# Layer 1 of a two-layer kernel: gating split between VectorE and GpSimd, expert sums on TensorE, and a changed order of the steps around the first and the last batches

## The chip, the core and the metric

The kernel runs on one core of a Trainium2 chip. The core has five engines, each with an instruction stream of its own that it runs in order: TensorE (PE: matrix products and transposes, with PEld for its weight loads), VectorE (DVE), ScalarE (ACT: activations), GpSimd (POOL) and SyncE (SP), which here only issues DMAs. They wait for each other through semaphores. The metric is the device time of one execution in microseconds, and the figure to compare is the median of several runs: 1055.69 us for the kernel before (3 runs, 1055.5 to 1057.73).

## What is computed

Two transformer layers over x of 8 batches x 512 tokens x 128 features, all in float32. Each layer has a mixer and a feed-forward part, both behind a layer norm that is modulated by a conditioning vector. Layer 0 is attention with low-rank weights and a mixture of experts (8 experts, 2 chosen for a token, and a shared one). Layer 1, where the change lies, is a selective state-space mixer and another mixture of experts. Cut to that:

```python
# mixer of layer 1: conv over time, projections, a linear recurrence
proj = conv(h) @ Win + b_in
delta, B_in, C = proj[..., :16], pairs_mean(proj[..., 16:48]), pairs_mean(proj[..., 48:])
dA = softplus(delta) * A                  # A = -exp(A_log)
A_bar = exp(dA)
B_bar = where(abs(A) < eps, 1 + dA / 2 + dA * dA / 6, (A_bar - 1) / A_safe) * B_in
h_t = A_bar_t * h_(t-1) + B_bar_t         # scan over 512 tokens
x = x + ga * ((C * h) @ Wout + b_out)

# feed-forward of layer 1
xc = silu(pw(conv(h)) + pw_b)
x1 = h + xc
top_v, top_i = top_k(x1 @ router_w + router_b, 2)
rw = one_hot(top_i) * softmax(top_v)      # two gates for a token, six are zero
ye = silu(x1 @ expert_w + expert_b)       # all 8 experts
moe_out = sum_e(rw[e] * ye[e]) @ out_w + out_b
h = rmsnorm(x1 + moe_out, norm_w)
x = x + gb * (h + gelu(h @ ff_down + b) @ ff_up + b2)
```

## The kernel before

Attention of layer 0 runs up to about 540 us of the profiled span and is not touched. Then a **loop over 62 blocks** does the experts of layer 0: 31 routed blocks of 256 tokens for batches 0 to 5, twelve blocks of the shared expert, fifteen routed blocks for batches 6 and 7 and their four shared ones. A pass of the loop, a *tick*, issues the transposes of the block after next, the first products of this block (`ph`, L1033, and the GELU to `hid` on ACT), and the second products of the block before (`pyb`, L1044). What layer 1 needs is put between the ticks: `when(t, do, ...)` hangs a step on tick t. `n` is 62, so ticks from n on come after the loop, and there the steps themselves are all the work. Ticks set only the order of each engine's stream; they are no times. Everything is pinned to the order in which the program issues it.

The results of routed blocks go to DRAM (`y_rows`) and come back by indirect DMAs that POOL issues, 8 per batch (`gather`, L1064); `combine` adds them on DVE. Then a batch takes these steps:

- **Mixer.** Statistics, root, centring, transposes to channels, and a convolution on DVE (`xc`). `ssm_project` (L1246) does the projections of pairs of batches; three ACT copies bring `dl`, `bi`, `ci` from PSUM. The groups (0, 1, 2, 3), (4, 5) and (6, 7) then go through a chain of seven steps: `chain_1` (L1274: bias and minus the absolute value on DVE, then exponential and logarithm on ACT), `chain_2` (on POOL the terms of the series, on ACT the exponential), `chain_3` (DVE), `chain_4` (the scan on DVE). Each switch between the tables of ACT is an instruction of its own (`ACT_TABLE_LOAD`).
- **Lead-in** (`lead_in`, L1579) for every batch: `ssm_out` (products `py`, L1327), statistics, `ffn_root` (L1336; POOL raises the variance to the power -0.5), `ffn_centre` (ACT), `ffn_channels` (transposes `ptn`), `ffn_pointwise` (L1348: products `pw`; for batches 0 to 3 SiLU is made of a hyperbolic tangent on ACT and two DVE operations into a tile `sl`, for the others it is ACT's own; POOL adds to get `x1`), `ffn_logits` (`pl`, L1371), `ffn_ranks` (comparisons on DVE, and the product `rk_eq` on POOL), `ffn_chosen`, `ffn_tanh`, `ffn_gates`, and `ffn_gates_out` (transposes `pgt`, a copy, and a DMA of the 8 x 512 gates to DRAM). The helper `later` turns estimated microseconds into ticks of 4.0 us in the loop and 2.2 us after it.
- **Experts.** `ffn_spread` (SP) reads a pair of rows of gates back, broadcast to all partitions (`gb`, 512 KB each, five buffers). For each of 8 experts `expert_in` (L1451) makes a product `pe` on PE and SiLU on ACT (`ye`), three ticks later `expert_gate` multiplies by the gates (`t`, five buffers), and `expert_sum` (L1441 in `add_up`) lets PE apply the output weights and sum the experts in PSUM (`r`). How many experts are added up on POOL before that, `sums_of` says: 2 for batches 0 to 3, 4 for batches 4 to 6, 1 for batch 7.
- **End.** Root mean square, the small feed-forward (`pf`, `pu`), and the output DMA, for batches 0 to 3 together between the experts of batches 5 and 6, then for 4 to 6, then for 7.

The first tick of a batch's experts is set by

```python
base = [n + 5 + NE * b + (5 if b > 5 else 0) for b in range(B)]
```

Of the kernel before, what the change touches and what calls it, by code (L numbers as in the profile page):

```python
# [14 lines left out]
ALU = mybir.AluOpType  # L15
# [53 lines left out]
def tile_adaln_two_blocks(  # L69
# [222 lines left out]
    with tc.tile_pool(name="at", bufs=2) as at, tc.tile_pool(name="sc", bufs=4, space=PSUM) as psc, tc.tile_pool(  # L292
# [953 lines left out]
        def ssm_project(h, s):  # L1246

            if s == 0:
                for name in ("dl", "bi", "ci"):
                    held[name] = lt([P, S], name)[0 : 16 * len(GROUPS[h]), :]  # L1250
            ps = flat(bank("pj"))
            for i in range(2):
                xc = held.pop(("xc", GROUPS[h][2 * s + i]))
                for k in range(3):
                    pin(
                        T.matmul(
                            ps[32 * k : 32 * k + 32, :],
                            lhsT=k1["wip"][:, k, i, :],
                            rhs=xc,
                            start=(i == 0),  # L1260
                            stop=(i == 1),
                        )
                    )
            for k, name in enumerate(("dl", "bi", "ci")):
                A.copy(held[name][32 * s : 32 * s + 32, :], ps[32 * k : 32 * k + 32, :])
# [8 lines left out]
        def chain_1(h, step):  # L1274

            dl = held["dl"]
            if step == 0:
                V.tensor_scalar(dl, dl, of_states(h, "bias"), None, ALU.add)
                u = chained(h, "u")
                V.scalar_tensor_tensor(u, dl, -1.0, dl, ALU.mult, ALU.min)  # L1280
            else:
                u = held["u"]
                A.activation(u, u, AF.Exp)
                A.activation(u, u, AF.Ln, bias=ones[0 : 16 * len(GROUPS[h]), 0:1])
# [63 lines left out]
        def ffn_pointwise(b):  # L1348
# [4 lines left out]
            x1 = flat(lt([P, NC4, D], "x1", tag="sh", bufs=B))  # L1353
            sl = lt([P, S], "sl", tag="xc", bufs=2)
            if b in GROUPS[0]:

                th = lt([P, S], "th", tag="gt1", bufs=2)
                A.activation(th, pw, AF.Tanh, bias=k1["pwb2"], scale=0.5)
                V.tensor_scalar(sl, pw, k1["pwb"], 0.5, ALU.add, ALU.mult)
                V.scalar_tensor_tensor(sl, th, 1.0, sl, ALU.add, ALU.mult)  # L1360
            else:
                A.activation(sl, pw, AF.Silu, bias=k1["pwb"])
            G.tensor_tensor(x1, hq[:, 2 : S + 2], sl, ALU.add)
            x1s[b] = x1
# [62 lines left out]
        def sums_of(b):  # L1427

            return 2 if b < 4 else 4 if b < B - 1 else 1

# [27 lines left out]
        def expert_gate(b, e):  # L1458
            f = ffn[b]
            t = f["t", e] = er.tile([P, S], FP, tag="t", name="t", bufs=5)  # L1460
            V.tensor_tensor(t, f.pop(("ye", e)), f["g"][e // 2][:, e % 2, :], ALU.mult)
            n = 1
# [115 lines left out]

        def lead_in(b, t):  # L1579

            when(t, ssm_out, b)
            for i in range(2):
                when(later(t, 2 * i + 1) if t >= n else t, two_stats, b, mv4, i)
            for do, us in (
                (ffn_root, 4), (ffn_centre, 8), (ffn_channels, 12), (ffn_pointwise, 16), (ffn_logits, 22),
                (ffn_ranks, 24), (ffn_chosen, 28), (ffn_tanh, 30), (ffn_gates, 32), (ffn_gates_out, 36),
            ):
                when(later(t, us), do, b)

        base = [n + 5 + NE * b + (5 if b > 5 else 0) for b in range(B)]  # L1590
        for b in range(B):
# [3 lines left out]
        for b in range(B):  # L1595
            t = base[b]
            for e in range(NE):
                when(t + e + 3, expert_gate, b, e)
            for i in range(NE // 2):
                when(max(t - 3 + 2 * i, n + 5), ffn_spread, b, i)  # L1600
            when(t - 1, ffn_residual, b)
            when(t + 5, ffn_bias, b)
            every = sums_of(b)
            lag = 4 if every == 1 else 5 if every == 2 else 6
            when(t + every - 1 + lag, sum_begin, b)
# [17 lines left out]
        for b, ts in enumerate(  # L1623
# [3 lines left out]
                (41, 42, 43, 44, 45, 46, 49),  # L1627
                (43, 44, 45, 46, 47, 48, 50),
                (46, 47, 48, 49, 50, 51, 52),
                (49, 50, 51, 52, 53, 54, 55),  # L1630
            )
# [12 lines left out]
        when(44, ssm_project, 0, 0)  # L1644
        when(49, ssm_project, 0, 1)
        when(53, out_weights, 0)
        chain(0, 50, (0, 0, 1, 2, 3, 3, 4))
        for b in GROUPS[0]:
            lead_in(b, 55 + b)
        when(59, ssm_project, 1, 0)  # L1650


        for k in range(2 * PC[1]):
            when(n - 2 + k // 3, gather, PB[0] + k // 8, k % 8)
        when(n + 8, out_weights, 1)
        chain(1, n + 5, (0, 1, 2, 4, 6, 7, 8))
        lead_in(4, n + 14)
        lead_in(5, n + 18)
        for b, t in ((6, n + 10), (7, n + 13)):
            for c in range(NC4):  # L1660
# [8 lines left out]
            when(t + 11, ssm_channels, b)  # L1669
        when(n + 20, out_weights, 2)  # L1670
        when(n + 27, ssm_project, 2, 0)
        chain(2, n + 28, (0, 1, 2, 4, 6, 7, 8))
        lead_in(6, n + 37)
        lead_in(7, n + 44)

# [111 lines left out]
```

## Time and profile before

| | us |
|---|---|
| median of 3 runs (1055.5 to 1057.73) | 1055.69 |
| the profiled execution | 1081.55 |
| its span, from first to last instruction | 1079.6 |
| PE busy in the span (93%) | 1004.6 |
| DVE busy (62%) | 668.8 |
| ACT busy (59%) | 637.0 |
| POOL busy (45%) | 486.7 |
| last products of the loop of layer 0 end at | 861.1 |
| first expert of layer 1 on PE begins at | 870.9 |
| first gated product on DVE begins at | 885.0 |
| first expert of batches 1, 2, 3, 4 begins at | 893.9 (with the last of batch 0), 919.9, 948.5 (with the last of batch 2), 972.8 (with the last of batch 3) |
| first expert of batch 6 begins at | 1030.9 |

The profile is one execution with the hardware's profiler on. A group of instructions is given with its line, engine, operation and tiles, how often it ran, its busy time, the mean length of one, and the idle time of its engine just before it with what ended that. L65 stands for most operations, as a helper records them; there the tiles tell which one it is. A matmul in float32 is two passes, so each `T.matmul` appears as two records. PE runs them in a pipeline: the mean length of one is longer than the distance from one to the next. A busy share is an average over stages with different limits, and the clock granted to PE (1.0 is full) differs by stage as well. The profiled execution is 25.9 us longer than the median of the runs.

### The profile page before, as it was taken

The numbers are of one execution on the slowest core, as the hardware profiler recorded it, in microseconds if no ns is written. First come the engines' busy times: TensorE is split into PE (matmuls) and PEld (weight loads), VectorE is DVE, ScalarE is ACT, GpSimd is POOL, SyncE is SP. The second block draws the span as 40 slices with busy tenths as digits, with TensorE's granted clock in tenths as the row PEclk, the third lists the DMA queues.
The fourth block names the chain that finished last, engine by engine and source line by source line (L and its number), as shares of the span: only waits on it lengthen the run. The fifth ranks groups of instructions, "written<-read, shape, count | busy, mean of one in ns | idle before, by whom it ended". The sixth has DMA issues, their size and how long they took to land.

```text
span 1079.6 us, 24180 instructions
## 1 busy us (share of the span) xinstructions
PE 1004.6 (93%) x9522; PEld 658.2 (61%) x9522; DVE 668.8 (62%) x1297; ACT 637.0 (59%) x1400; POOL 486.7 (45%) x764
## 2 busy tenths in 40 slices
PE   9999999999999999999989999869899967767988
PEld 7555555555555555555579899748778634344556
DVE  6967787777768777777321123035766359888663
ACT  1466676666767666676745656225586563675554
POOL 3313142554627445454453133546441374666662
PEclk9999999999999999999999999969999968999999
DMA  6099200000000000000237796412553043213051
GB/s 168 20 315 283 88 12 2 11 22 2 31 1 20 13 9 24 2 30 10 71 114 221 230 275 196 127 35 64 146 152 89 8 131 99 79 59 126 23 186 39
DMA packets 94769, 95.36 MB, mean 88 GB/s; under 512 B 7664, under 2 KB 72560, under 8 KB 94656
## 3 DMA queue, kind: packets, MB, share of 16 engines
q1 hardware_dynamic: 90384, 85.13, 26.4%
q0 software_dynamic: 4096, 8.40, 2.6%
q8 instruction: 75, 1.23, 0.5%
q10 hardware_dynamic: 176, 0.30, 0.1%
q14 instruction: 38, 0.31, 0.1%
HBM read 62.43 MB, written 31.36 MB: 87 GB/s over the span
## 4 chain that ended last, share of the span: by engine, by line
PE 75%; DVE 10%; POOL 5%; ACT 4%; issue 4%; DMA 1%; SPq 0%; DVEq 0%; ACTq 0%; POOLq 0%
PE ps L531 21%; PE av L552 11%; PE pyb L1044 9%; PE ph L1033 8%; PE pm L484 3%; PE pmt L519 2%; PE r L1441 2%; PE pw L1352 2%; PE ppt L570 2%; DVE t L65 1%; DVE xc L65 1%; PE idle L417 1%; PE pe L1453 1%; PE pqk L444 1%; PE pyb L1003 1%
## 5 line engine op out<-in xcount | busy, mean ns | idle before, releaser
L65 DVE TENSOR_REDUCE mpad<-pm 128x2 f32<-128x1024 f32 (+1 forms) x262 | 310.3, 1194 | 110.2 <-PE pm L484 107.1
L65 ACT ACTIVATE es<-ps 128x512 f32<-128x512 f32 x512 | 275.6, 598 | 158.7 <-PE pm L484 135.0
L531 PE MATMUL ps<-qt,kt 32*128 32x512 f32 x1024 | 291.2, 630 | 0.7 <-DVE x L65 0.6
L484 PE MATMUL pm<-kt,qt 32*128 32x512 f32 x976 | 261.5, 636 | 0.0
L552 PEld LDWEIGHTS av<-es,vaug 128*32 128x32 f32 x4096 | 104.2, 109 | 94.1 <-ACT part L65 42.5
L552 PE MATMUL av<-es,vaug 128*32 128x128 f32 x4096 | 137.7, 276 | 0.0
L531 PEld LDWEIGHTS ps<-qt,kt 32*128 32x128 f32 x1024 | 94.0, 183 | 61.4 <-issue 30.6
L65 ACT ACTIVATE hid<-ph,bias 128x256 f32<-128x256 f32 x184 | 72.3, 478 | 58.0 <-PE ph L1033 56.2
L786 POOL DMA_INDIRECT x_rows<-tok,ux x64 | 65.0, 1015 | 68.4 <-DMA x_rows<-tok,ux 61.8
L1044 PEld LDWEIGHTS pyb<-w2b,hid 128*128 128x128 f32 x736 | 91.1, 194 | 5.8 <-ACT hid L65 2.4
L1044 PE MATMUL pyb<-w2b,hid 128*128 128x128 f32 x736 | 91.9, 278 | 2.6 <-ACT hid L65 2.0
L1033 PE MATMUL ph<-xt,w1b 128*128 128x256 f32 x368 | 89.9, 388 | 1.7 <-issue 1.7
L1064 POOL DMA_INDIRECT yg<-y_rows,yrows x64 | 63.3, 989 | 38.1 <-DMA hl<-h_chan 19.0
L484 PEld LDWEIGHTS pm<-kt,qt 32*128 32x128 f32 x976 | 73.1, 183 | 8.7 <-ACT kf L65 5.4
L1453 PE MATMUL pe<-x,l1w_sb 128*128 128x512 f32 x128 | 70.4, 663 | 5.3 <-ACT ye L65 5.3
L1033 PEld LDWEIGHTS ph<-xt,w1b 128*128 128x128 f32 x368 | 68.3, 195 | 9.8 <-issue 2.1
L65 DVE COPY xt<-pxt 128x256 f32<-128x256 f32 x46 | 19.2, 419 | 88.8 <-PE pxt L958 77.2
L65 POOL TENSOR_SCALAR qt<-qf,mask,zero 128x512 f32<-128x512 f32 x31 | 23.9, 772 | 109.4 <-PE pm L484 92.9
L65 ACT ACTIVATE ye<-pe,pc 128x512 f32<-128x512 f32 x64 | 43.2, 684 | 36.9 <-PE pe L1453 34.6
L65 POOL TENSOR_TENSOR t<-t 128x512 f32<-128x512 f32 x34 | 48.0, 1413 | 23.3 <-DVE t L65 21.8
L65 DVE TENSOR_TENSOR t<-ye,gb 128x512 f32<-128x512 f32 x64 | 55.0, 882 | 2.6 <-POOL t L65 2.3
L1441 PE MATMUL r<-l1w_sb,t 128*128 128x128 f32 x240 | 34.3, 290 | 15.2 <-POOL t L65 11.9
(298 smaller groups left out, 1559.4 us busy)
## 6 DMA issues: line engine op xcount, KB each, us to landing
x_rows<-zeros SPq DMA_DIRECT2D x16, 1024.0 KB
gb<-g_rows SPq DMA_DIRECT2D x32, 512.0 KB
w1b<-in_w1t SPq DMA_DIRECT2D x46, 256.0 KB
w2b<-in_w2t SPq DMA_DIRECT2D x46, 256.0 KB
xg<-x_rows SPq DMA_DIRECT2D x46, 128.0 KB
y_rows<-yb SPq DMA_DIRECT2D x46, 128.0 KB
x<-in_x SPq DMA_DIRECT2D x8, 256.0 KB
h_chan<-hf SPq DMA_DIRECT2D x8, 256.0 KB
```

The lines of the kernel that those rows point to most:

```text
L65: return lambda *args, **kwargs: self.pin(call(*args, **kwargs))
L484: T.matmul(pm[:, i, :], lhsT=qt[r : r + 32, qc * P : (qc + 1) * P], rhs=kt[r : r + 32, :], start=True, stop=True,)
L519: pin(T.transpose(pt[:, c, :], mpads[g % 4][:, c, :], ident))
L531: T.matmul(ps, lhsT=kt[r : r + 32, kc * P : (kc + 1) * P], rhs=qt[r : r + 32, :], start=True, stop=True)
L552: T.matmul(ps[32 * j : 32 * j + 32, 0, :], lhsT=vaugs[b % 2][:, kc, 4 * j + m, :], rhs=es_of[4 * g + kc, j][:, q], start=(kc == 0), stop=( ...
L570: pin(T.transpose(pt[:, c, :], part[:, c, :], ident))
L786: nc.gpsimd.indirect_dma_start(out=x_rows[h], out_offset=IndirectOffsetOnAxis(ap=chosen["ux", b][:, k, c : c + 1], axis=0), in_=half[h]["t ...
L1033: pin(T.matmul(ph[:, f, :], lhsT=it["w1"][:, f * P : (f + 1) * P], rhs=it["x"], start=True, stop=True))
L1044: T.matmul(py[:, c, :], lhsT=it["hid"][:, f, c * P : (c + 1) * P], rhs=it["w2"][:, f, :], start=(f == 0 and "shared" not in it), stop=(f = ...
L1064: nc.gpsimd.indirect_dma_start(out=gathered[b][:, k, c, :], out_offset=None, in_=y_rows[h], in_offset=IndirectOffsetOnAxis(ap=half[h]["yro ...
L1441: T.matmul(ffn[b]["r"][:, c, :], lhsT=x[:, c * P : (c + 1) * P], rhs=w, start=(start and c == 0), stop=stop, skip_group_check=True,)
L1453: pin(T.matmul(pe, lhsT=l1w_sb[:, 2 + e, :], rhs=x1s[b], start=True, stop=True))
```

## The change

The edits, all in layer 1:

1. **Gating.** For batches 0 to 3 the products with gates of odd experts are made on POOL rather than DVE. `sums_of` is 1 for them, so POOL adds no pairs, and PE sums all eight.
2. **Chain.** The bias of `dl` is added in the ACT pass that brings it from PSUM. `chain_1` takes the absolute value on ACT (with a scale of -1 in the exponential) and has no DVE operations left.
3. **x1.** SiLU is written to the tile of `x1` itself, and POOL adds in place. The tile `sl`, which shared two buffers with `xc`, is gone.
4. **Order of steps to the first gates.** `lead_in` takes a list of lags. Batches 0 to 3 begin at tick 53 + b instead of 55 + b, with lags (1, 1, 2, 3, 5, 5, 6, 6, 7, 8); from the start of batch 0's lead-in to its gates it is 8 ticks rather than 11. In the loop `ssm_project` of batches 2 and 3 and chain 0 come a tick earlier, chain 0 takes 3 ticks rather than 4, and the mixer steps of batches 3 to 5 move by a tick (batch 3 earlier, 4 and 5 later).
5. **Ticks after the loop.** Experts begin at n rather than n + 5, and the gap before batch 6 is 3 ticks rather than 5. Chain 1, the lead-ins of batches 4 and 5, and the mixer of 6 and 7 come 3 to 5 ticks earlier. A spread of gates comes no earlier than a tick after the gates have been written (`out_at`).
6. **Gathers.** Of batches 6 and 7, the first eight gathers come in ticks n - 3 to n - 1, three a tick, and the others one a tick from n + 3 to n + 10. Before, all sixteen came from n - 2 to n + 3, three a tick.

```diff
--- before.py
+++ after.py
@@ -1261,7 +1261,10 @@
                             stop=(i == 1),
                         )
                     )
-            for k, name in enumerate(("dl", "bi", "ci")):
+            A.activation(
+                held["dl"][32 * s : 32 * s + 32, :], ps[0:32, :], AF.Identity, bias=k1["bias"][32 * s : 32 * s + 32, 0:1]
+            )
+            for k, name in ((1, "bi"), (2, "ci")):
                 A.copy(held[name][32 * s : 32 * s + 32, :], ps[32 * k : 32 * k + 32, :])
 
         def chained(h, name, tag=None):
@@ -1273,14 +1276,11 @@
 
         def chain_1(h, step):
 
-            dl = held["dl"]
             if step == 0:
-                V.tensor_scalar(dl, dl, of_states(h, "bias"), None, ALU.add)
-                u = chained(h, "u")
-                V.scalar_tensor_tensor(u, dl, -1.0, dl, ALU.mult, ALU.min)
+                A.activation(chained(h, "u"), held["dl"], AF.Abs)
             else:
                 u = held["u"]
-                A.activation(u, u, AF.Exp)
+                A.activation(u, u, AF.Exp, scale=-1.0)
                 A.activation(u, u, AF.Ln, bias=ones[0 : 16 * len(GROUPS[h]), 0:1])
 
         def chain_2(h, step):
@@ -1351,16 +1351,15 @@
             for t in range(3):
                 pin(T.matmul(pw, lhsT=k1["pwk"][:, t, :], rhs=hq[:, t : t + S], start=(t == 0), stop=(t == 2)))
             x1 = flat(lt([P, NC4, D], "x1", tag="sh", bufs=B))
-            sl = lt([P, S], "sl", tag="xc", bufs=2)
             if b in GROUPS[0]:
 
                 th = lt([P, S], "th", tag="gt1", bufs=2)
                 A.activation(th, pw, AF.Tanh, bias=k1["pwb2"], scale=0.5)
-                V.tensor_scalar(sl, pw, k1["pwb"], 0.5, ALU.add, ALU.mult)
-                V.scalar_tensor_tensor(sl, th, 1.0, sl, ALU.add, ALU.mult)
+                V.tensor_scalar(x1, pw, k1["pwb"], 0.5, ALU.add, ALU.mult)
+                V.scalar_tensor_tensor(x1, th, 1.0, x1, ALU.add, ALU.mult)
             else:
-                A.activation(sl, pw, AF.Silu, bias=k1["pwb"])
-            G.tensor_tensor(x1, hq[:, 2 : S + 2], sl, ALU.add)
+                A.activation(x1, pw, AF.Silu, bias=k1["pwb"])
+            G.tensor_tensor(x1, hq[:, 2 : S + 2], x1, ALU.add)
             x1s[b] = x1
 
         def ffn_logits(b):
@@ -1426,7 +1425,7 @@
 
         def sums_of(b):
 
-            return 2 if b < 4 else 4 if b < B - 1 else 1
+            return 4 if 4 <= b < B - 1 else 1
 
         def ffn_residual(b):
 
@@ -1458,7 +1457,8 @@
         def expert_gate(b, e):
             f = ffn[b]
             t = f["t", e] = er.tile([P, S], FP, tag="t", name="t", bufs=5)
-            V.tensor_tensor(t, f.pop(("ye", e)), f["g"][e // 2][:, e % 2, :], ALU.mult)
+            on = G if b < 4 and e % 2 else V
+            on.tensor_tensor(t, f.pop(("ye", e)), f["g"][e // 2][:, e % 2, :], ALU.mult)
             n = 1
             while 2 * n <= sums_of(b) and (e + 1) % (2 * n) == 0:
                 G.tensor_tensor(t, f.pop(("t", e - n)), t, ALU.add)
@@ -1576,18 +1576,25 @@
             for (do, *args), i in zip(steps, lags):
                 when(t + i, do, h, *args)
 
-        def lead_in(b, t):
+        out_at = {}
+
+        def lead_in(b, t, lags=None):
 
             when(t, ssm_out, b)
             for i in range(2):
                 when(later(t, 2 * i + 1) if t >= n else t, two_stats, b, mv4, i)
-            for do, us in (
-                (ffn_root, 4), (ffn_centre, 8), (ffn_channels, 12), (ffn_pointwise, 16), (ffn_logits, 22),
-                (ffn_ranks, 24), (ffn_chosen, 28), (ffn_tanh, 30), (ffn_gates, 32), (ffn_gates_out, 36),
+            out_at[b] = t + (lags[-1] if lags else later(t, 36) - t)
+            lags = lags or [later(t, us) - t for us in (4, 8, 12, 16, 22, 24, 28, 30, 32, 36)]
+            for do, i in zip(
+                (
+                    ffn_root, ffn_centre, ffn_channels, ffn_pointwise, ffn_logits,
+                    ffn_ranks, ffn_chosen, ffn_tanh, ffn_gates, ffn_gates_out,
+                ),
+                lags,
             ):
-                when(later(t, us), do, b)
-
-        base = [n + 5 + NE * b + (5 if b > 5 else 0) for b in range(B)]
+                when(t + i, do, b)
+
+        base = [n + NE * b + (3 if b > 5 else 0) for b in range(B)]
         for b in range(B):
             t = base[b]
             for e in range(NE):
@@ -1596,12 +1603,10 @@
             t = base[b]
             for e in range(NE):
                 when(t + e + 3, expert_gate, b, e)
-            for i in range(NE // 2):
-                when(max(t - 3 + 2 * i, n + 5), ffn_spread, b, i)
-            when(t - 1, ffn_residual, b)
+            when(max(t - 1, n), ffn_residual, b)
             when(t + 5, ffn_bias, b)
             every = sums_of(b)
-            lag = 4 if every == 1 else 5 if every == 2 else 6
+            lag = 4 if b == last else 5 if every == 1 else 6
             when(t + every - 1 + lag, sum_begin, b)
             for e in range(every - 1, NE, every):
                 when(t + e + lag, expert_sum, b, e)
@@ -1625,9 +1630,9 @@
                 (36, 37, 38, 39, 40, 41, 47),
                 (38, 39, 40, 41, 42, 43, 48),
                 (41, 42, 43, 44, 45, 46, 49),
-                (43, 44, 45, 46, 47, 48, 50),
-                (46, 47, 48, 49, 50, 51, 52),
-                (49, 50, 51, 52, 53, 54, 55),
+                (42, 43, 44, 45, 46, 47, 50),
+                (47, 48, 49, 50, 51, 52, 54),
+                (50, 51, 52, 53, 54, 57, 58),
             )
         ):
             for c in range(NC4):
@@ -1642,21 +1647,21 @@
                 when(ts[5], ssm_conv, b, i)
             when(ts[6], ssm_bias, b)
         when(44, ssm_project, 0, 0)
-        when(49, ssm_project, 0, 1)
-        when(53, out_weights, 0)
-        chain(0, 50, (0, 0, 1, 2, 3, 3, 4))
+        when(48, ssm_project, 0, 1)
+        when(51, out_weights, 0)
+        chain(0, 49, (0, 0, 1, 1, 2, 2, 3))
         for b in GROUPS[0]:
-            lead_in(b, 55 + b)
+            lead_in(b, 53 + b, (1, 1, 2, 3, 5, 5, 6, 6, 7, 8))
         when(59, ssm_project, 1, 0)
 
 
         for k in range(2 * PC[1]):
-            when(n - 2 + k // 3, gather, PB[0] + k // 8, k % 8)
-        when(n + 8, out_weights, 1)
-        chain(1, n + 5, (0, 1, 2, 4, 6, 7, 8))
-        lead_in(4, n + 14)
-        lead_in(5, n + 18)
-        for b, t in ((6, n + 10), (7, n + 13)):
+            when(n - 3 + k // 3 if k < 8 else n - 5 + k, gather, PB[0] + k // 8, k % 8)
+        when(n + 3, out_weights, 1)
+        chain(1, n, (0, 1, 2, 4, 6, 7, 8))
+        lead_in(4, n + 9)
+        lead_in(5, n + 13)
+        for b, t in ((6, n + 6), (7, n + 10)):
             for c in range(NC4):
                 when(t + c, combine, b, c)
             when(t + 4, combine, b, NC4)
@@ -1667,11 +1672,15 @@
             when(t + 9, ssm_centre, b)
             when(t + 10, ssm_bias, b)
             when(t + 11, ssm_channels, b)
-        when(n + 20, out_weights, 2)
-        when(n + 27, ssm_project, 2, 0)
-        chain(2, n + 28, (0, 1, 2, 4, 6, 7, 8))
-        lead_in(6, n + 37)
-        lead_in(7, n + 44)
+        when(n + 16, out_weights, 2)
+        when(n + 24, ssm_project, 2, 0)
+        chain(2, n + 25, (0, 1, 2, 3, 5, 6, 7))
+        lead_in(6, n + 33)
+        lead_in(7, n + 40)
+
+        for b in range(B):
+            for i in range(NE // 2):
+                when(max(base[b] - 3 + 2 * i, n, out_at[b] + 1), ffn_spread, b, i)
 
 
         LAST = 2 * STEPS + 8
```

## What I expect the change to do

> **What bounds the kernel now.** I read the summary first: TensorE (PE) is busy for 93% of the span, but that is an average over unlike stages. So I took the busy time of the engines in stretches, cut where the edits lie: the expert blocks of layer 0 up to 861 us, the lead-in to the first expert of layer 1 (871), batch 0 (894), batches 1 to 3 (973), 4 and 5 (1011), then the rest. Columns: us, then busy us of PE, weight loads, VectorE (DVE), ScalarE (ACT), GpSimd (POOL), then TensorE's granted clock, DMA share, GB/s.
>
> ```profile
> 784.00:861.00 77.00, 74.48 (x467) 60.86 (x466) 44.17 (x124) 51.78 (x112) 24.70 (x34) 0.98 0.30 86
> 861.00:871.00 10.00, 7.20 (x38) 5.43 (x37) 7.14 (x22) 2.02 (x5) 7.79 (x9) 0.81 0.10 27
> 871.00:894.00 23.00, 14.99 (x44) 7.14 (x44) 14.24 (x26) 16.44 (x22) 18.14 (x18) 0.71 0.47 150
> 894.00:973.00 79.00, 57.63 (x258) 35.21 (x258) 68.40 (x143) 45.59 (x97) 45.72 (x47) 0.94 0.24 78
> 973.00:1011.00 38.00, 32.09 (x126) 18.07 (x125) 28.74 (x58) 20.45 (x46) 25.35 (x23) 0.91 0.31 98
> 1011.00:1031.00 20.00, 19.94 (x115) 13.37 (x114) 12.42 (x23) 12.40 (x27) 12.03 (x12) 1.00 0.23 62
> ```
>
> PE is the bound up to 861 (97% busy). From 861 to 973 it is not: it has 2.8, 8.0 and 21.4 us without work, and runs at clock 0.71 in batch 0. DVE is busy for 87% of batches 1 to 3. That is the stretch in which a change of gating can pay. At 1011 to 1031 PE is full again.
>
> Second, the waits between 860 and 1080 (us in total, times, longest):
>
> ```profile
> POOL t L65 <- DVE t L65: 21.8, 11, 6.2
> PEld r L1441 <- POOL t L65: 16.0, 9, 4.9
> PE r L1441 <- POOL t L65: 11.9, 6, 4.1
> ACT z L65 <- DVE z L65: 9.2, 3, 4.6
> DVE rk_gt L65 <- POOL rk_eq L65: 8.4, 2, 5.9
> ```
>
> The sums on PE (`r`) wait for POOL's pair sums (`t`), which wait for DVE's gated products. And DVE's ranking waits for one POOL product, `rk_eq`. Why, POOL's order of time shows:
>
> ```profile
> 875.02 0.95 POOL L1064 DMA_INDIRECT yg<-y_rows,yrows  x1 [0.30 <-issue]
> 875.99 0.73 POOL L65 TENSOR_TENSOR rk_eq<-rk_eq,tri 128x256 f32<-128x256 f32 x1
> 876.88 1.16 POOL L1064 DMA_INDIRECT yg<-y_rows,yrows  x1 [0.16 <-issue]
> ```
>
> `rk_eq` stands behind six gathers, the next behind four, at 1.25 us each. DVE stood 5.9 and 2.5 us, ACT behind it 4.6, and the first gated product came at 885.0, though its gates had left for DRAM at 871.8.
>
> **1. Gating (batches 0 to 3).** Per batch: four of eight products go from DVE to POOL, POOL's four pair sums go, and PE sums eight terms instead of four. The rows:
>
> ```profile
> L65 DVE TENSOR_TENSOR t<-ye,gb 128x512 f32<-128x512 f32 x64 | 55.0, 882 | 2.6 <-POOL t L65 2.3 <-POOL futg L65 0.3
> L65 POOL TENSOR_TENSOR t<-t 128x512 f32<-128x512 f32 x34 | 48.0, 1413 | 23.3 <-DVE t L65 21.8 <-DVE var L65 1.0
> ...
> 1038.13 10.81 DVE L65 TENSOR_TENSOR t<-ye,gb 128x512 f32<-128x512 f32 x8
> ...
> 1042.87 4.92 POOL L65 TENSOR_TENSOR t<-t 128x512 f32<-128x512 f32 x3 [1.30 <-DVE t L65]
> ```
>
> POOL: 16 sums out, 16 products of the same form in (two inputs, 128x512), so nothing. DVE: 16 x 0.882 = 14.1 us out. A product's path to PE also loses one link: DVE then POOL became POOL alone.
>
> Here a rule speaks against it. The Trainium skill, GPSIMD Engine Reference, "Engine selection", keeps two-input elementwise work on VectorE, GpSimd being about 2x slower; the rows agree (medians 1.27 against 0.68 us), and on that rule alone 16 products cost 16 x 0.59 = 9.4 us more. But POOL's removed sums pay for them, so it decides nothing. Harder is SBUF — State Buffer, "SBUF: two separate sides": a DVE operation with two SBUF inputs and a GpSimd operation that reads SBUF lock each other out for the whole instruction. The fourth fence shows it: eight products of 0.68 us took 10.81 us while POOL worked beside them. By the rule the pair's time is what counts, per batch 8 x 0.68 + 4 x 1.27 = 10.5 us before and 4 x 0.68 + 4 x 1.27 = 7.8 after: 2.7 x 4 = 10.9 us. By the DVE row it is 14.1; the least is 16 x 0.60 (the pitch of undisturbed products) = 9.6. These stages are 81% covered by DVE (82.6 of 102 us), so 0.81 x 10.9 = **-9 us**; ends -2 (the freed time is waited away elsewhere) and -14.
>
> PE: 16 more sums of 4 products in two passes. Their mean of 290 ns counts overlap; the pitch is in the chain that ended last:
>
> ```profile
> 1049.91 1.78 PE r L1441 x16
> ```
>
> 0.111 us each, so 16 x 8 x 0.111 = 14.2 us. They lie in 871 to 973, where PE has 29.4 us free; but a PE in order can use a hole only where its sum is ready, so **+3 us**; ends 0 and +14.2.
>
> **2. Way to the first gates.** Lead-ins 0 to 3 start 2 ticks (blocks of the loop) earlier with closer steps. One pointwise product (2.6 us), three of logits (0.8 each) and one transpose of gates (0.45) move in front of the last block, on a full PE: the loop ends 5.5 us later, near 866.6, and the first expert follows at once instead of at 870.9: **-4 us**. Gates 0 leave for DRAM before the loop's last block, so the spreads (SP, next in its queue) land by then, and the first product waits only for its table load and activation, near 869 against 885. In batch 0 stay chain 1's table loads (1.28 us each). Of the 16 us that DVE and ACT gain, batch 0's experts can take what makes its 23 us the pace of batches 1 to 3 after part 1, some 17: **-6 us**; ends 0 and -15.
>
> Against it, in the loop: the reciprocal root on POOL (1.0 us) and its use now share a tick, so DVE stands for POOL four times, and ACT's centring (1.65 us) precedes the next hidden activations. From 820 to 861 DVE was busy 18.3 and ACT 24.1 of 41 us, which hides it; chain 0 also has five blocks to run in rather than six, and there PE had already waited 2.05 us for ACT. **+1.5 us**; ends 0 and +19 (rival C). Chain: three bias additions and minima (0.47 + 0.68 us on DVE) become one ACT pass (0.63), and no wait for `xc` buffers remains before x1: **-1 us** (0 to -4).
>
> **3. Gathers.** Batches 6 and 7: eight before the loop's end, eight one a tick. The 16 still cost 20 us of POOL, now between products; a POOL product that waits for its activation holds up the gathers behind it. The last one is issued three ticks before combine 7 reads it (ten before): should POOL run later than that, DVE stands, at 1.25 us a gather. I take nothing (0 to +3): POOL has 23.3 us of idle time before its sums. What `rk_eq` no longer waits for is counted in 2.
>
> **4. Ends.** Batch 6 and 7's experts follow their gates by 4 and 5 ticks instead of 7 and 8. Writing gates to DRAM and spreading them took from 1024.0 to the first spread's issue at 1026.1 and its transfer, some 5 us; a tick without other work can be 2. **+2 us** (0 to +6). The gap of 5 ticks before batch 6 is PE work (19.9 of 20 us), so making it 3 gains nothing.
>
> Sum: -9 + 3 - 4 - 6 + 1.5 - 1 + 2 = -13.5. The profiled execution took 1081.55 us (span 1079.6 and 2 around it), 26 above the median; it holds stalls without a cause at 695 to 717 us, outside what is changed. So I carry the difference: 1055.7 - 13.5 = **1042 us**.
>
> **Rivals.**
> A. DVE was the whole bound, and every gain arrives: -14 - 4 - 15 - 1 + 3 = -31, **1025 us**. For it: 87% DVE, clock 0.71 in batch 0. Against: ACT's table loads remain.
> B. PE takes over: the 14.2 us of sums fall on a full PE and eat the gating: -13.5 + 11.2, **1053 us**. For it: PE is 73% busy there, by 79 us at that, and each sum now waits for a POOL product by itself. Against: holes of 29 us.
> C. Slower. In the PE-bound loop the closer steps come up late: each of 12 PE steps (transpose, pointwise, logits, four batches) waits for DVE, ACT and POOL. At 1.6 us each (a root and its hop) 19 us: -15 + 19 = +4, **1060 us**. It decides from 1.3 us a step. For it: PE has no slack at 820 to 861. Against: py to transpose takes DVE 4.7 and ACT 1.65 us, and has two blocks of over 4.
> That the edits do not take effect is excluded: the engines' programs differ as described.
>
> **Chances.** Forecast (1034 to 1050) 0.45, A 0.17, B 0.15, C 0.23. Differences of 0.2% (2.1 us) are about what measurement can tell from none. B splits 0.07 faster, 0.05 same, 0.03 slower: faster 0.69, same 0.05, slower 0.26. Range 1022 to 1061: A whole, the unknown ends, and C's centre; above it and below it some 0.15 is left.
>
> **What would show it.** Right: first gated product before 872; no DVE wait for `rk_eq` over 2 us; batches 0 to 3 (first expert to batch 4's) under 92 us rather than 102; PE over 80% in them. Wrong: last loop product after 872 (C); waits of PE for `t` above 28 us, or PE full from 870 to 960 (B); a wait of DVE for spreads of batch 6 (part 4).

## The result and the profile after

The changed kernel takes 1047.93 us (median of 4 runs, 1046.61 to 1049.18) against 1056.71 us for the kernel before in the same comparison (4 runs, 1055.5 to 1057.96). The ratio is 0.9913, with a 95% interval of 0.989 to 0.9935: 9 us faster, where 13.5 had been forecast. The profiled execution has a span of 1046.8 us and took 1048.89, close to the median; that of the kernel before was 25.9 us above its own. One place accounts for most of that: a single pass of layer 0's loop took 22.6 us in it (693.5 to 716.1) and 4.5 here. So the two traces are compared only behind that place. I cut both at the start of the second products (`pyb`) of the same block, fourteen blocks from the loop's end (785.0 us before, 760.3 after, so 24.7 lie between the two scales), and from there on at the first expert of each batch:

| stretch, us | before | after | difference |
|---|---|---|---|
| last 14 blocks of the loop | 76.3 | 82.8 | +6.5 |
| end of the loop to the first expert | 9.6 | -0.2 | -9.8 |
| batch 0 | 23.9 | 21.1 | -2.8 |
| batches 1, 2, 3 | 25.1, 29.5, 24.2 | 21.3, 26.1, 27.9 | -3.5 |
| batches 4 and 5 | 57.2 | 52.9 | -4.3 |
| batch 6 to the end | 48.7 | 54.6 | +5.9 |
| sum (rows are rounded) | 294.6 | 286.5 | -8.1 |

Now the same stages in the profile after, by busy time in stretches (columns as before: us, then PE, weight loads, DVE, ACT, POOL, granted clock, DMA share, GB/s). The rows are batch 0 and the four batches together:

```profile
842.90:864.00 21.10, 15.61 (x63) 9.35 (x62) 9.12 (x15) 17.95 (x25) 11.57 (x12) 0.84 0.48 163
...
842.90:939.20 96.30, 79.17 (x414) 52.66 (x413) 66.07 (x143) 64.70 (x124) 63.13 (x65) 0.95 0.30 102
```

The four batches together before:

```profile
870.90:973.70 102.80, 73.42 (x302) 42.68 (x302) 83.30 (x169) 62.60 (x120) 64.62 (x65) 0.89 0.29 94
```

DVE is busy for 17 us less, POOL for 1.5 less, and the time has come down by 6.5. What holds up these batches, if not DVE's busy time? Four lines of the list of waits from 820 us to the end (total, times, longest), which are not neighbours in it:

```profile
POOL da L65 <- DVE dl L65: 15.8, 2, 8.6
PEld r L1440 <- POOL t L65: 13.7, 9, 5.3
DVE dl L65 <- ACT u L65: 9.5, 2, 5.1
PE r L1440 <- POOL t L65: 8.3, 6, 4.4
```

PE still waits for `t` from POOL, 13.7 and 8.3 us where it was 16.0 and 11.9. The ranking's wait for `rk_eq` is gone from the list. A new chain stands in its place: POOL's `da` waits for `dl`, DVE's `dl` waits for ACT. In batch 3 one sees what hangs on it. First POOL in order of time, then PE:

```profile
919.37 1.73 POOL L65 TENSOR_TENSOR t<-ye,gb 128x512 f32<-128x512 f32 x1
928.32 1.55 POOL L65 TENSOR_SCALAR da<-dl,asm 32x512 f32<-32x512 f32 x1 [7.21 <-DVE dl L65]
...
933.05 1.26 POOL L65 TENSOR_TENSOR t<-ye,gb 128x512 f32<-128x512 f32 x1
```

```profile
934.36 1.42 PE L1440 MATMUL r<-l1w_sb,t 128*128 128x128 f32 x8 [4.43 <-POOL t L65]
```

POOL idles for 7.2 us with a gated product queued behind `da`, and PE idles for 4.4 us behind that product. ACT in batch 0 shows why `dl` is late (in batch 3 it goes through the same five steps at 923.55 to 928.82):

```profile
848.27 1.28 ACT L65 ACT_TABLE_LOAD   x1
849.56 0.63 ACT L65 ACTIVATE u<-u 32x512 f32<-32x512 f32 x1
850.21 1.28 ACT L65 ACT_TABLE_LOAD   x1
851.50 0.72 ACT L65 ACTIVATE u<-u,ones 32x512 f32<-32x512 f32 x1
852.24 1.28 ACT L65 ACT_TABLE_LOAD   x1
853.54 0.69 ACT L65 ACTIVATE ye<-pe,pc 128x512 f32<-128x512 f32 x1
```

Before the next SiLU, ACT spends 5.3 us on two operations of the chain and three table loads. `dl` needs the second operation, so it waits for two of the loads; the experts' SiLU waits for all three.

### The profile page after: what moved, and what is told of

Same layout as the page of the kernel before. It is cut to its first block, busy times and chain, and to the rows that moved or that the text cites. A ratio compares the mean times of both kernels' runs of the same rounds, so it can differ in the third digit from the quotient of the medians.

```text
span 1046.8 us, 24415 instructions
## 1 busy us (share of the span) xinstructions
PE 1003.1 (96%) x9650; PEld 662.2 (63%) x9650; DVE 658.5 (63%) x1275; ACT 638.0 (61%) x1403; POOL 486.3 (46%) x764
## 4 chain that ended last, share of the span: by engine, by line
PE 76%; DVE 10%; POOL 5%; ACT 4%; issue 2%; DMA 2%; SPq 0%; ACTq 0%; POOLq 0%; DVEq 0%
PE ps L531 22%; PE av L552 11%; PE pyb L1044 9%; PE ph L1033 8%; PE pm L484 3%; DVE xc L65 2%; PE r L1440 2%; PE pe L1452 2%; PE pmt L519 2%; PE ppt L570 2%; PE pqk L444 1%; PE idle L417 1%; DVE sh L65 1%; PE pw L1352 1%; ACT L65 1%
## 5 line engine op out<-in xcount | busy, mean ns | idle before, releaser
L1064 POOL DMA_INDIRECT yg<-y_rows,yrows x64 | 66.8, 1043 | 35.9 <-issue 17.8
L65 DVE COPY xt<-pxt 128x256 f32<-128x256 f32 x46 | 19.2, 419 | 76.2 <-PE pxt L958 76.2
L1440 PEld LDWEIGHTS r<-l1w_sb,t 128*128 128x128 f32 x368 | 47.9, 197 | 28.8 <-POOL t L65 13.7
L1440 PE MATMUL r<-l1w_sb,t 128*128 128x128 f32 x368 | 50.7, 283 | 10.8 <-POOL t L65 8.3
L65 DVE TENSOR_TENSOR t<-ye,gb 128x512 f32<-128x512 f32 x48 | 41.8, 892 | 1.8 <-DMA gb<-g_rows 0.9
```

The costliest lines, as they stand in the source:

```text
L65: return lambda *args, **kwargs: self.pin(call(*args, **kwargs))
L1064: nc.gpsimd.indirect_dma_start(out=gathered[b][:, k, c, :], out_offset=None, in_=y_rows[h], in_offset=IndirectOffsetOnAxis(ap=half[h]["yro ...
L1440: T.matmul(ffn[b]["r"][:, c, :], lhsT=x[:, c * P : (c + 1) * P], rhs=w, start=(start and c == 0), stop=stop, skip_group_check=True,)
```

## The experiments

In the comparisons below the kernel before took 1083 to 1085 us instead of 1056, and the profiles of all twelve kernels have the long pass of layer 0's loop (22 to 27 us). So each is read as a ratio to the kernel before in the same comparison, and its profile only behind that pass. An interval is about 0.2% each way, 2 us. The changed kernel was not run again in these comparisons: its 0.9913 is carried over from the first one (the kernel that differs from it least, with five ticks ahead of batch 6, had 0.9914). The fourteenth block before the loop's end begins at 780 to 786 us in the twelve profiles, though hardly anything is changed ahead of it; so a time and a profile can differ by a few us, and a reading is firm where both agree. The theories: **G**, the gating edit is worth what the prediction said; **O**, the order of steps is worth everything; others are named where they are tested.

### The two halves of the change, and of the gating edit

**Gating alone** on the kernel before:

```diff
-            return 2 if b < 4 else 4 if b < B - 1 else 1
+            return 4 if 4 <= b < B - 1 else 1
...
-            V.tensor_tensor(t, f.pop(("ye", e)), ...)
+            on = G if b < 4 and e % 2 else V
+            on.tensor_tensor(t, f.pop(("ye", e)), ...)
...
```

(The last line left out keeps the lag from expert to sum at the five ticks that it was for these batches.)

> The kernel before with the gating edit only: batches 0 to 3 make odd products on POOL, PE sums all eight experts; order, gathers and chain as before. Theory G (gating is worth what the prediction says, -9 on DVE and +3 on PE): 6 us faster than before, ratio 0.994. Rival O (the change's 9 us come from the order of steps alone; the products that stand behind POOL's gathers and chain steps eat the gating): within 2 us of before, ratio 0.998 to 1.002. Rival S (the 16 sums fall on a full PE): 5 us slower, 1.005.

Measured: 0.9999 (0.9981 to 1.0018). The edit by itself does nothing that can be seen: the prediction's -9 + 3 = -6 us are not there. G falls.

**The change without the gating edit** (the same lines undone in the changed kernel):

> The changed kernel with the gating edit undone: all products on DVE, pair sums on POOL for batches 0 to 3, everything else as changed. Theory G: the changed kernel's 0.9913 plus 6 us, ratio 0.997. Rival O: stays at 0.991. Rival S: better than the changed kernel, 0.986.

Measured: 0.991 (0.9891 to 0.9929), the changed kernel's 0.9913. In both orders the gating edit as a whole is worth nothing, as O expected: the gain belongs to the other edits. But an edit worth nothing can be a gain and a loss, so its halves were parted.

**All products on DVE, all sums on PE**, in the changed kernel:

```diff
-            on = G if b < 4 and e % 2 else V
+            on = V
```

> The changed kernel with all gated products on DVE and still all sums on PE: POOL loses 16 products of 1.27 us, DVE gets 16 of 0.68 us. If DVE's own busy time is the bound of batches 0 to 3 (the prediction's -9): 16 x 0.68 = 11 us more on DVE, 6 to 9 us over the changed kernel, ratio 0.997 to 1.000. If what counts is the time in which DVE and POOL lock each other out (per batch 8 x 0.68 = 5.4 us here against 4 x 0.68 + 4 x 1.27 = 7.8): 2.4 us a batch less, 0.985 or so. If neither is the bound of these batches any more: 0.991.

Measured: 0.9809 (0.9788 to 0.9829), 1% or 11 us better than the changed kernel. Half the products on POOL, against all on DVE, are a loss.

**Sums on PE alone**, on the kernel before:

```diff
-            return 2 if b < 4 else 4 if b < B - 1 else 1
+            return 4 if 4 <= b < B - 1 else 1
...
```

> The kernel before with one edit: batches 0 to 3 have no pair sums on POOL, PE sums all eight experts, all products stay on DVE. Theory P (POOL in the path of the gating is what costs, whatever it does there; the first experiments gave 11 us for taking it out of the changed kernel): 11 us faster than before, ratio 0.990. Rival D (in the order of before, DVE is 87% busy and stands for the ranking product, so the sums give nothing until the order is changed): 0.998 to 1.001. The prediction's own term for these sums, +3 us: 1.003.

Measured: 0.9889 (0.9862 to 0.9917), 12 us better than before. Theory P holds and D falls. This edit takes the pair sums off POOL and puts the eight sums on PE at once, so it doesn't measure the prediction's +3 for PE by itself. With these the table is complete (in brackets the profile from the fourteenth block before the loop's end to the end, us):

| ratio to the kernel before | order of before | changed order |
|---|---|---|
| products on DVE, pair sums on POOL | 1 (294.6) | 0.991 (288.8) |
| half the products on POOL, sums on PE | 0.9999 (297.8) | 0.9913 (286.5) |
| products on DVE, sums on PE | 0.9889 (287.0) | 0.9809 (278.4) |

The columns differ by 0.8 to 0.9% in each row, and the rows by the same in both columns, within the intervals. So the parts add: the pair sums moved from POOL to PE are a gain of 11 to 12 us, the products moved to POOL a loss of 11 to 12, the rest of the change a gain of 9. The profiles have the same signs and a little less for the first two, 8 to 10 and 8 to 11 us.

The profiles of batches 0 to 3 (first expert to batch 4's) show how. In this order: gating alone, sums alone (both in the order of before), and all products on DVE in the changed order:

```profile
871.50:976.90 105.40, 84.36 (x414) 55.55 (x413) 75.45 (x161) 63.90 (x123) 62.46 (x67) 0.89 0.28 92
```

```profile
870.30:965.40 95.10, 80.50 (x415) 53.77 (x414) 71.99 (x173) 63.54 (x123) 48.40 (x53) 0.94 0.30 102
```

```profile
865.70:950.60 84.90, 75.79 (x415) 51.69 (x413) 60.90 (x151) 61.70 (x114) 44.57 (x50) 0.98 0.35 114
```

With gating alone DVE is busy for 7.9 us less (75.5 for 83.3) and the stretch is no shorter, 105.4 for 102.8: DVE's busy time was not its bound. And the second row has sixteen products *more* on DVE than the first, some 11 us, yet DVE is busy for *less*: 72.0 against 75.5. The work that left DVE came back as longer DVE operations beside a busier POOL. Which operations depends on what meets POOL's in time. In the order of before it is the two `bs` of the chain, here with gating alone and then with sums alone (busy us, mean ns, idle before):

```profile
L65 DVE TENSOR_SCALAR bs<-ab,inva 32x512 f32<-32x512 f32 x2 | 8.8, 4414 | 2.4 <-ACT ab L65 2.4
```

```profile
L65 DVE TENSOR_SCALAR bs<-ab,inva 32x512 f32<-32x512 f32 x2 | 3.2, 1597 | 0.5 <-POOL ts L65 0.5
```

The six operations of the convolution of batches 6 and 7 take 0.90 us each in both of these. In the changed order it is they that grow; first the changed kernel, then all products on DVE:

```profile
L65 DVE SCALAR_TENSOR_TENSOR xc<-hq,pc,xc 128x511 f32<-128x511 f32 x6 | 7.8, 1300 | 0.3
```

```profile
L65 DVE SCALAR_TENSOR_TENSOR xc<-hq,pc,xc 128x511 f32<-128x511 f32 x6 | 4.5, 748 | 0.3
```

1.30 us each against 0.75; the first of them runs for 1.65 us from 900.35 on, while POOL has a product from 899.99 to 901.45. As an estimate from the first two rows of stretches, each product on POOL saved DVE 0.68 us and cost it 0.9 elsewhere ((16 x 0.68 + 3.5) / 16).

The sums on PE are the other side of it. PE's groups in batches 0 to 3, both in the changed order: first without the gating edit (pair sums on POOL), then with all products on DVE and all sums on PE:

```profile
L1452 PE MATMUL pe<-x,l1w_sb 128*128 128x512 f32 x65 | 36.6, 669 | 4.5 <-ACT ye L65 4.5
L1440 PE MATMUL r<-l1w_sb,t 128*128 128x128 f32 x104 | 16.9, 314 | 16.5 <-POOL t L65 13.6 <-POOL hq L65 1.6 <-POOL xc L65 1.3
```

```profile
L1452 PE MATMUL pe<-x,l1w_sb 128*128 128x512 f32 x65 | 34.4, 612 | 5.7 <-ACT ye L65 5.7
L1440 PE MATMUL r<-l1w_sb,t 128*128 128x128 f32 x216 | 29.2, 279 | 0.1
```

The added sums cost 12.3 us of PE time, where the prediction had 14.2. But PE no longer idles before them (16.5 us to 0.1), and the expert products take 2.2 us less. PE's idle time in the stretch goes from 27.8 to 9.1 us, and in the order of before from 29.4 to 14.6: the holes were not only room for the sums, they were in good part made by what the sums replaced.

### Queue or lock?

Two mechanisms could make a product on POOL dear: its place in POOL's queue (behind `da`), and the lock between DVE and POOL. **The series terms later:** in the changed kernel the four POOL operations of the chain are issued with the chain's second exponential, a tick or two later, behind the gated product that they blocked in batch 3:

```diff
             if step == 0:
                 V.scalar_tensor_tensor(dl, dl, 0.0, u, ALU.max, ALU.add)
-                da = chained(h, "da")
-                G.tensor_scalar(da, dl, of_states(h, "asm"), None, ALU.mult)
...
             else:
                 A.activation(chained(h, "ab"), dl, AF.Exp, scale=of_states(h, "an"))
+                da = chained(h, "da")
+                G.tensor_scalar(da, dl, of_states(h, "asm"), None, ALU.mult)
...
```

> The changed kernel with the four POOL operations of the chain's series (da and three of ts) issued with the exponential of the chain, one or two ticks later, so that no gated product on POOL stands behind da while da waits for ACT's three table loads. Theory Q (what the POOL products cost is their place in POOL's queue): the 4.4 and the 2 us that PE stood for t in batches 3 and 0 go, and what hangs on them: 5 to 9 us under the changed kernel, ratio 0.983 to 0.987. Rival L (what they cost is that DVE and POOL lock each other out while both work; DVE's busy time in batches 0 to 3 was 66 us with them and 61 without, though it then made 16 products more): no change, 0.990 to 0.992.

Measured: 0.9851 (0.983 to 0.9873), 0.6% or 7 us better than the changed kernel, the size that Q expected. But the profile doesn't bear this out. Batches 0 to 3 are 6.5 us shorter there:

```profile
863.10:952.90 89.80, 76.90 (x415) 52.42 (x413) 61.95 (x137) 61.45 (x114) 59.61 (x63) 0.96 0.31 108
```

Yet batches 4 and 5 take 57.2 us instead of 53.0 and the rest 55.4 instead of 54.6, so that 1.5 us are left from the first expert on. The wait has moved rather than gone: another product of batch 3 now stands behind `da`, and PE waits for it just behind the cut. POOL, then PE:

```profile
946.89 1.55 POOL L65 TENSOR_SCALAR da<-dl,asm 32x512 f32<-32x512 f32 x1 [5.74 <-DVE dl L65]
...
956.31 1.63 POOL L65 TENSOR_TENSOR t<-ye,gb 128x512 f32<-128x512 f32 x1
```

```profile
958.00 2.08 PE L1440 MATMUL r<-l1w_sb,t 128*128 128x128 f32 x8 [4.01 <-POOL t L65]
```

So theory Q is not shown. Leaving POOL out altogether gains 11 us by the times and 9 by the profiles from the first expert on; this edit gains 7 by the times and 1.5 by the profiles. Between the two kernels lie 4.5 or 7 us; POOL is busy for 15 us more there, and the six operations of the convolution still take 1.30 us each, as the lock would have it, but no run tested the lock by itself. In the order of before the loss is of the same size, though `da` waits only 5.1 us in all and PE 3.6 us for `t`: there the queue behind `da` can't be the whole of it. How the loss divides between queue and lock stays open.

### The rest of the change

**Gathers back in a burst**, in the changed kernel:

```diff
-            when(n - 3 + k // 3 if k < 8 else n - 5 + k, gather, PB[0] + k // 8, k % 8)
+            when(n - 2 + k // 3, gather, PB[0] + k // 8, k % 8)
```

> The changed kernel with the gathers of batches 6 and 7 where they were: all sixteen in ticks n-2 to n+3, three a tick. The prediction took spreading at nothing: ratio 0.991. Rival: in the changed order the first gated products of batch 0 on POOL, chain 1's terms on POOL and two ranking products stand behind eight more gathers at 1.25 us each, up to 10 us in a stretch where PE has no other work: 5 us or more over the changed kernel, 0.996 or above.

Measured: 0.993 (0.9911 to 0.9948), 0.17% or 2 us over the changed kernel, less than the two intervals. By the profile batch 0 takes 28.7 us instead of 21.1, batches 1 and 4 give 5.4 of it back (18.2 and 16.4 us instead of 21.3 and 18.7), and the whole from the first expert on is 4.8 us longer.

**Gathers alone**, the reverse edit on the kernel before:

> The kernel before with the gathers of batches 6 and 7 spread as in the change, nothing else. The first eight still come in the loop's last three ticks, the other eight one a tick. Theory: DVE's 8.4 us of waiting for the ranking product, and ACT's 4.6 us behind it, go, and the first gated product comes 5 us or more earlier; as ACT's table loads set batch 0 anyway, 2 to 5 us of it reach the end: ratio 0.995 to 0.998. Rival, as the prediction took it (nothing by itself): 0.999 to 1.001.

Measured: 0.9972 (0.9958 to 0.9987), 3 us. Spreading is a gain by itself. Batch 0 takes 20.6 us there instead of 23.9, the whole from the first expert on 205.4 instead of 208.7, and the first gated product comes 9.4 us behind the first expert instead of 14.1.

**The chain and x1 edits alone**, on the kernel before:

> The kernel before with two of the edits: the chain's bias and absolute value on ACT, and SiLU written to the tile of x1. The prediction has -1 us for both (0 to -4): ratio 0.999, 0.996 at the least. Rival (three ACT operations of 0.63 us come into batch 0, where ACT is busy for 16.4 of 23 us and the experts wait for it): +1 to +2 us, 1.001 to 1.002.

Measured: 1.0011 (1.0 to 1.0022): no gain, at most a small loss. The Rival's size fits, but the interval begins at 1.

**The order alone**, the changed kernel with the gating edit undone and the gathers in a burst:

> The changed kernel with neither gating edit nor spread gathers: what is left is the order of steps (lead-ins, ticks after the loop, spreads of gates) with the chain and x1 edits. By the prediction -4 - 6 + 1.5 - 1 + 2 = -7.5 us against before: ratio 0.993. If the spread gathers belong to the way to the first gates: 0.996 or above, while the kernel with spread gathers too had 0.991. If the order is worth all: 0.991.

Measured: 0.9955 (0.9939 to 0.9971), 5 us; with the spread gathers 0.991. So of the 9 us of the table's right column some 4 to 5 are the gathers and 5 the order. Without the spread batch 0 took 27.5 us here:

```profile
867.10:894.60 27.50, 14.39 (x47) 7.44 (x47) 12.88 (x18) 17.14 (x23) 22.40 (x22) 0.77 0.48 167
```

POOL is busy for 22.4 of them. Experts that begin 10 us earlier behind the loop run into the gathers, and part of the earlier start is waited away.

**Five ticks ahead of batch 6** instead of three, in the changed kernel:

```diff
-        base = [n + NE * b + (3 if b > 5 else 0) for b in range(B)]
+        base = [n + NE * b + (5 if b > 5 else 0) for b in range(B)]
```

> The changed kernel with five ticks, not three, ahead of the experts of batch 6, so that batches 6 and 7 follow their gates by two ticks more. The prediction has +2 us for the shorter way from gates to products, and nothing for the gap: 2 us under the changed kernel, ratio 0.989. Rival (the shorter gap is a gain, as batches 5 to 6 took 34.2 us instead of 38.3): 2 to 4 us over it, 0.993 to 0.995. If both are hidden: 0.991.

Measured: 0.9914 (0.9892 to 0.9936): the same. Batch 5 takes 39.8 us instead of 34.2 and batch 6 9.6 instead of 14.9; the edit only moves the cut between them.

### Further?

**All sums on PE**: all products on DVE, and `sums_of` is 1 for every batch.

> The changed kernel with all products on DVE and the sums of all batches on PE, so POOL is in no path of the gating: for batches 4 to 6 PE gets 18 more sums of 0.89 us (16 us), of which 7 to 8 lie in stretches where it is full. If the gain of batches 0 to 3 carries over (PE stands for t of POOL there as well): 3 us under the kernel with this edit for batches 0 to 3 alone, which had 0.981, so 0.978. If PE is the bound of batches 4 to 6: 5 us or more over it, 0.986.

Measured: 0.9838 (0.9816 to 0.986), 3 us over the kernel with this edit for batches 0 to 3 alone, with intervals that overlap. Between the two expectations: batches 4 to 7 take 115.4 us instead of 110.2 there, PE being busy for 107 of them. The gain doesn't carry over to batches in which PE has fewer holes (14 us in these 110.2; 27.8 in the 98.3 of batches 0 to 3 before their sums came to PE).

**A shorter chain on ACT**: all products on DVE, and the second exponential right behind the logarithm, four table loads a chain instead of five.

```diff
-        chain(1, n, (0, 1, 2, 4, 6, 7, 8))
+        chain(1, n, (0, 1, 1, 1, 6, 7, 8))
-        chain(2, n + 25, (0, 1, 2, 3, 5, 6, 7))
+        chain(2, n + 25, (0, 1, 1, 1, 5, 6, 7))
```

> The best kernel so far (the changed one with all products on DVE, 0.981) with the chain's second exponential issued right behind the logarithm in the chains of batches 4 to 7, so that ACT goes from exponential to logarithm to exponential and back to SiLU: four table loads of 1.28 us a chain instead of five, and ACT waits some 1 us for DVE's dl. If ACT bounds batch 0 there (17.8 of 19.2 us busy, PE 14.1): 1 to 3 us less, 0.978 to 0.980. If PE's wait only moves: 0.981.

Measured: 0.9785 (0.9764 to 0.9806). That is the lowest of all, 23 us under the kernel before, but it can't be told from 0.9809: the intervals overlap, and the profile speaks against a gain, as batch 0 takes 21.5 us instead of 19.2 and the part behind the loop's end 196.7 instead of 194.9. That either of the two beats both the kernel before and the changed one is clear; which is the better isn't.

## Why the prediction came out as it did

The forecast was 1042 us, the measurement 1047.93, inside its range; the gain was two thirds of the one forecast. That it came so near is in part luck. The gating's -6 us were not there, and the gathers, put at nothing, brought 2 to 5. The order of steps with the chain, forecast at -7.5, brought 5.

- **Gating, -9 on DVE and +3 on PE.** This step failed: together they measured 0, in both orders. "POOL: 16 sums out, 16 products of the same form in (two inputs, 128x512), so nothing" counts POOL's time and not its queue: a product stands in order behind whatever POOL waits for, and the chain's `da` waits 7 to 9 us for `dl`. And "These stages are 81% covered by DVE" took a busy share for a bound: DVE's busy time fell by 7.9 us and the stretch was no shorter.
- **What it did not compare.** The edit is two moves, pair sums from POOL to PE and products from DVE to POOL. The prediction weighed only the two ends, by the lock of the Trainium skill's SBUF — State Buffer, "SBUF: two separate sides": 10.5 us a batch before, 7.8 after. The same sum for the kernel between them, with nothing of the gating on POOL, is 8 x 0.68 = 5.4. So the rule itself made the first move a gain of 5.1 us a batch and the second a loss of 2.4, for four batches -20 and +10 (estimates from the prediction's own figures). Measured: -11 to -12 and +11 to +12. The signs are right, but the two cancel, where the rule leaves some -11. The rule was applied to products and pair sums alone, while POOL's busy time was 64.6 us before and 62.5 with gating alone, so that DVE's other operations met it as before; and it has no queue in it. Which of the two the missing 11 us are is open. GPSIMD Engine Reference, "Engine selection", was put aside because the removed sums paid for it; its choice, these products on DVE, was the better one, by 11 to 12 us where its factor alone gave 9.4.
- **PE sums, +3.** The 14.2 us were sized about rightly (12.3 in the trace). But the holes that should have hidden them were in good part PE's own waits for POOL's pair sums, and they went with them. I had mentioned the lost link under the gating and given it no number.
- **Way to the first gates, -4, -6 and +1.5.** For the loop and the gap behind it the sum was right: the loop's end comes 6.5 us later (5.5 + 1.5 forecast) and the gap of 9.6 us is gone. The first gated product was forecast 2.4 us behind the loop's end and comes 9.8 behind it (23.7 before). Two queues were overlooked. The spread of gates was not next in SP's: the first gates left at 840.3, then SP wrote batch 1's gates at 846.6, and the spread was issued at 847.2. And DVE's stream had `dl` ahead of the product, waiting for ACT (whether the gates had landed by then the trace doesn't say):

```profile
852.25 0.68 DVE L65 SCALAR_TENSOR_TENSOR dl<-dl,u 32x512 f32<-32x512 f32 x1 [5.12 <-ACT u L65]
852.86 0.67 DVE L65 TENSOR_TENSOR t<-ye,gb 128x512 f32<-128x512 f32 x1
```

  Of batch 0's 6 us 2.8 arrived; its ACT is busy for 17.95 of 21.1 us, the chain's five table loads among them, which were named as what stays.
- **Gathers, 0.** Too low: 3 us alone, 4 to 5 in the changed order without the gating edit; with it 2 by the times, within the intervals, and 5 by the profile. They were what batch 0 would have waited for next.
- **Chain, -1** measured +1 at most. **Ends, +2**: batch 5 to the end took 87.0 us before and 88.8 after, and no product of batches 6 and 7 waited over 0.9 us for its gates. Two more ticks gained nothing, so the 1.8 us are not the short way.
- **Tests set beforehand.** First gated product before 872: missed. The trace has it at 852.9, but on the scale of the trace before, 24.7 us on, that is 877.6. No wait for `rk_eq` over 2 us: met. Batches 0 to 3 under 92 us: missed (96.3), and this pointed at the gating. PE over 80% in them: met (82%). Last loop product after 872: no, 867.8 on the same scale. Rival A (DVE the whole bound) and rival C (the loop pays 19 us; it paid 6.5, of which the prediction had put 5.5 down to work that moved there) are out. Rival B's 1053 is a little nearer to the measurement than the forecast, but not for its reason: the sums on PE didn't eat a gain of the gating, they were its gain.

## What to carry to other kernels

Moving an operation between engines is priced by what it stands behind in the new queue and by what it holds up there, not by its duration alone; where one operation is exchanged for another on a shared engine, compare with leaving that engine out altogether. A busy share near 90% is not yet a bound while other engines hold up or feed that one: take the work away on paper and ask which wait ends last then. When a wait goes from the stretch you look at, look for it behind the cut. And an edit that measures nothing may be a gain and a loss of the same size, so run its halves apart.

## What the hardware showed that I had not expected

- One pass of layer 0's loop took 22 to 27 us in the profiles of the kernel before and of all twelve experiments, and 4.5 in the changed kernel's. PE, ACT and DVE go slowly there while POOL issues gathers one behind the other; most of PE's gaps of 1 to 2.5 us have no releaser. That POOL issues them is not enough for it: in the changed kernel's profile it does so too, and from 692 to 718 us PE is busy throughout. One such gap, in the kernel with all products on DVE:

```profile
702.85 0.60 PE L1044 MATMUL pyb<-ws,hid 128*128 128x128 f32 x2 [2.20 <-issue]
```

  The kernel before itself took 1056 us in one comparison and 1083 to 1085 in the others, a difference of which this pass, 18 us longer in the kernel before than in the changed one, is the larger part; so it seems to depend on where or when a program runs, not on the change. No run here was made for it, and its cause is open.
- With fewer holes PE did its old work a little faster. The granted clock of batches 0 to 3 rose from 0.90 to 0.98 with the sums on PE (changed order) and from 0.89 to 0.94 (order of before), and the same 65 expert products took 34.4 us for 36.6 and 37.7 for 38.8. It is not the added work that does it: gating alone gave PE the same sums and left it at 0.89, with 21.0 us idle, where the others with the sums have 9.1 and 14.6. The Trainium skill, TensorE: Matmul & The Clock Gate, "Part 1: The HAM clock gate (the "warmup" mystery)", has activity as what releases the clock; these rows agree.
- A switch of ACT's tables cost its 1.28 us and no more: in the rows of ACT shown above, a load begins 0.02 us behind the end of the operation before it, and the next operation 0.01 to 0.02 us behind the load.
